# The LayerNorm bias product turned round, parts of layer 0 placed anew, and transposes of layer 1 spread over three PSUM homes

## The chip, the cores and the metric

One Trainium2 chip; the kernel runs on one core of it. The metric is the device time of one launch in microseconds (us), lower is better. The time before is 4759.32 us, the median of three runs (4757.85 to 4759.87).

## What is computed

Two layers over x of shape (2, 512, 64, 64), all in float32. Layer 0 is a Mamba layer on the 4096 tokens of each image, layer 1 matches each token with the rows of a memory of 1024 rows. Both work on a group norm of their input and add the result to it:

```python
x = x + mamba(gn(x), ln_w, ln_b, in_proj_w, conv_w, ...)
# mamba: xn = layernorm(x) * ln_w + ln_b;  xin, z = split(xn @ in_proj_w.T)
#        u = silu(conv4(xin) + conv_b);    dt, B, C = split(u @ x_proj_w.T)
#        delta = softplus(dt @ dt_proj_w.T + dt_proj_b)
#        h = exp(delta * A) * h + delta * u * B;  y = sum_n(h * C) + D * u   # along the tokens
#        out = (y * silu(z)) @ out_proj_w.T
x = x + memory(gn(x), m)
# memory: score = unit(x) @ unit(m).T;  idx = argmax(score)
#         new_m = 0.999 * m + 0.001 * (mean of the tokens of each row)
#         out = softmax(score) @ new_m
```

ln_w and ln_b are folded away: the weight `win` is multiplied by ln_w along its rows, and the vector `beta` = in_proj_w @ ln_b (from the unscaled weight) is added behind the projection.

## The kernel before, in words

**Layer 0.** Channels lie on the partitions; the tokens are cut into 32 chunks of 256 (16 for each image). A chunk has 32 *units*: 8 blocks `db` of 128 inner channels by 4 groups `g` of 4 state indices. One turn of the main loop handles unit k: `decay(k+1)` has ScalarE (ACT) write four exponentials into a PSUM tile `dA0` or `dA1`; `scan(k)` runs the recurrence on VectorE (DVE) over that tile; `weigh` multiplies by C (on DVE, or, for the units listed under `aside`, on GpSimd, POOL); `gather` has TensorE (PE) add the 8 transposed pieces into the PSUM tile `yT`; `feed(k+4)` has POOL write `bu` = B * du into one of four buffers, and `first(k+3)` has ACT write its first column. `start` prepares a pair of blocks on POOL, `turn` transposes the pair's sum back into the PSUM tile `py`, and `gate` multiplies by z.

All other work of a chunk (group norm, LayerNorm, in-projection `u_mm` and `z_mm`, convolution, softplus, out-projection) is cut into small parts, and the table `AT` says at which unit each part is issued; keys with a 1 at the end hold for chunk 1, whose front runs beside chunk 0. Layer 0 goes through `InOrder`: each engine executes its instructions in program order, so a part that waits holds up everything behind it on its engine. Layer 1's first half is not wrapped in this way, and its order on an engine can differ from the program's.

**Layer 0's start.** x is read once for the statistics of image 0 (16 loads `xl` of 512 KB through 8 buffers, DVE takes `bn_stats` of each), with the first half of `win` in the middle of these loads on SyncE's queue (SP). `affine_mm(0)` computes the first half of `beta` with `win` as the stationary operand: 8 blocks by 4 channel blocks, one moving column each. `affine_out(0)` copies it and scales that half of `win` on ACT. Behind it in program order come the end of the group statistics (`stats_end(0)`: `gs_pm`, `gs_pv` on PE, then `gsh`), the norms of chunk 0, its front, `affine_mm(1)` in two pieces, `feed(0)` to `feed(3)`, `decay(0)` and the loop. `affine_out(1)` is issued from the table at unit 0 and scales the second half of `win` on DVE; `z_mm` reads that half.

**Layer 1, first half.** Tokens come in tiles of 512, each in two pairs of 128-token sub-tiles. For a pair, seven half-size products (`product`, line 1224; the Strassen-Winograd form with banks A to D) give 256 by 1024 scores. `best` finds the row, `match` and `add_rows` add the token to a table in DRAM (gather, add, scatter through POOL's queue), `weights` and `scale` form the softmax `ex`, and `exT_part` transposes `ex` four blocks at a time into a PSUM bank, which ACT copies to `exT`. The transposes of earlier sub-tiles are done in steps 4, 5, 6 and 6 of a pair: three of them in the single bank `px`, the last one (`alt`) in the single bank `pt`, which `turn` also uses. The pool `pe` has two buffers, used by `match` (`pr`) and `add_rows` (`pe`).

**Layer 1, second half** (again in program order). `table_rows` loads both tables, 16 loads on ACT's queue; `new_m` forms a block of new memory rows on DVE; the first sums over the kept tiles `T[0]` (DVE) and `kept2` (POOL) are issued ahead of `new_m` on their engines; then products of 16 instructions follow each other on PE to the end.

Of the kernel before, what the change touches and what calls it, by code (L numbers as in the profile page):

```python
# [51 lines left out]
def kernel(  # L52
# [138 lines left out]
    with ExitStack() as l0:  # L191
# [5 lines left out]
            "u": (-10, -8, -3, 1), "xi": (-9, -6, 2, 2), "c": (-6, -2, 3, 5), "o": (-4, -1, 4, 7),  # L197
            "x": 10, "xo": 12, "z": (17, 18, 20, 23), "zo": (19, 20, 21, 24),
            "soft": (19, 21, 22, 22, 23, 24, 25, 26), "silu": 9, "aside": (0, 4, 8, 12, 16, 26),
            "gate": 2, "norm": (-3, 0, 2, 8, 9, 11, 12, 14, 16, 17, 18, 19),  # L200
            "back": ((0, 6, 8, 10, 12, 13), (1, 13, 14, 16, 17, 21)), "end": 23,
            "u1": (3, 5, 8, 9), "xi1": (4, 6, 9, 11), "c1": (6, 10, 11, 11),
            "o1": (8, 11, 12, 13), "x1": 14, "xo1": 16, "silu1": 13, "gate1": 7,
            "z1": (1, 1, 4, 5),
            "soft1": ((-7, -5, -4, -2, -1, 2, 3), (1, 4, 5, 5, 6, 8, 8), (7, 8, 8, 10, 18, 19, 19)),
            "wo": (6, -5, 8, 7), "m": (7, 12, 17, 24, 26, 29), "gs": 11, "zo1": (2, 4, 5, 6),
            "norm1": (0, 0, 0, 0, 0, 0, 0, 1, 1), "affine": 0,
            "aside_end": (2, 17, 21, 25, 27, 29),
# [38 lines left out]
        def win_load(h):  # L247
            nc.sync.dma_start(
                win[:, :, h * DI : (h + 1) * DI],
                in_wT[:, h * DI : (h + 1) * DI].rearrange("(cb p) j -> p cb j", p=P),  # L250
            )
# [115 lines left out]
        for n, xl in enumerate(stats_load(0)):  # L367
            big.append(xl)
            if n == CB * NQ // 2 - 1:
                win_load(0)  # L370
# [28 lines left out]
        pbs = {}  # L399

        def affine_mm(h, js=range(DB)):
            if js[0] == 0:
                pbs[h] = psy.tile([P, HT, 2, P], F32, tag="yT", name="pb")
                pbs[h] = pbs[h].rearrange("p a b q -> p (a b q)")
            pb = pbs[h]
            for j in js:
                for cb in range(CB):
                    nc.tensor.matmul(
                        pb[:, j : j + 1], win[:, cb, (h * DB + j) * P : (h * DB + j + 1) * P],
                        lnb[:, cb : cb + 1], start=cb == 0, stop=cb == CB - 1,  # L410
                    )

        def affine_out(h, cbs=range(CB)):
            if cbs[0] == 0:
# [633 lines left out]
        for k, (i, db, g) in enumerate(units):  # L1048
            w = k % U
            if k + 1 < n_units:  # L1050
                decay(k + 1)
# [528 lines left out]
```

## Time and profile before

The profiled execution took 4760.57 us, of which the span from its first to its last instruction is 4758.9 us.

| Stage | us from the span's start | PE busy | DVE busy | ACT busy | POOL busy |
|---|---|---|---|---|---|
| chunk 0 from its first scan | 98.30 to 206.00 | 94.56 | 74.30 | 76.60 | 84.76 |
| chunk 1 | 206.00 to 320.00 | 105.00 | 108.71 | 102.58 | 108.21 |
| a later chunk | 2461.41 to 2574.97 | 104.75 | 109.05 | 102.84 | 111.04 |
| layer 1, first half, a stretch | 3800 to 4000 | 193.72 | 164.12 | 102.60 | 96.90 |
| layer 1, second half, a stretch | 4400 to 4600 | 200.00 | 63.83 | 8.10 | 44.59 |

Times of one instruction stand on the page as "busy, mean ns"; "idle before" is what the engine waited just before the instruction, and the name behind the arrow is what ended that wait. A float32 matrix product is two instructions on PE, a transpose is one.

### The profile page before, as it was taken

What the parts mean: (1) busy time and instruction counts of PE and PEld (TensorE: products, weight loads), DVE (VectorE), ACT (ScalarE), POOL (GpSimd) and SP (SyncE); (2) the same over time, 40 slices, a digit from 0 to 9 for tenths busy, and PEclk for the clock granted to TensorE, in tenths of its full rate; (3) what the DMA queues carried; (4) which work ended last, traced back from release to release, by engine and by line L of the source; (5) the groups of instructions that cost most, each with busy time, mean ns of one, the idle gap of its engine ahead of it and who ended that gap; (6) DMA issues with size and microseconds to landing.
All of it is one profiled execution on the core that took longest, in us unless ns stands there. A gap on an engine that the chain in (4) does not pass through costs nothing. (4 is left out here: it accounts for less than half of the span.)

```text
span 4758.9 us, 65491 instructions
## 1 busy us (share of the span) xinstructions
PE 4364.2 (92%) x22644; PEld 3433.4 (72%) x22644; DVE 4157.1 (87%) x3498; ACT 3622.1 (76%) x9313; POOL 3959.6 (83%) x2664
## 2 busy tenths in 40 slices
PE   7899999999999999989999999999997699999999
PEld 6787788788877887878888878888786644454444
DVE  5799999999999999999999999999999888887322
ACT  3799899989999999889899899898988655553000
POOL 4799999999999999999999999999999744554212
PEclk9999999999999999999999999999998899999999
DMA  6132222222222222212222212222222134445442
GB/s 226 39 110 80 69 67 67 67 73 73 76 75 72 72 72 72 72 67 68 67 68 67 67 68 74 78 77 78 75 70 90 54 129 166 146 163 184 166 182 106
DMA packets 175363, 439.36 MB, mean 92 GB/s; under 512 B 23704, under 2 KB 78104, under 8 KB 171320
## 3 DMA queue, kind: packets, MB, share of 16 engines
q1 hardware_dynamic: 158072, 358.50, 22.2%
q10 hardware_dynamic: 6720, 42.08, 2.4%
q0 software_dynamic: 10240, 34.61, 2.2%
q8 instruction: 178, 2.92, 0.3%
q14 instruction: 153, 1.25, 0.1%
HBM read 347.44 MB, written 87.69 MB: 91 GB/s over the span
## 5 line engine op out<-in xcount | busy, mean ns | idle before, releaser
L38 POOL TENSOR_TENSOR bu<-B,du 128x1020 f32<-128x1020 f32 (+1 forms) x1151 | 2463.7, 2161 | 130.9 <-DVE dA L38 80.0
L38 ACT ACTIVATE dA<-delta,A 128x256 f32<-128x256 f32 x4096 | 1958.3, 478 | 131.9 <-DVE hc L38 25.6
L38 DVE TENSOR_TENSOR_SCAN dA<-dA,bu 128x1024 f32<-128x1024 f32 x832 | 1904.6, 2289 | 76.9 <-ACT dA L38 50.9
L38 PE MATMUL yT<-ident,hc 128*128 128x128 f32 x8192 | 1061.6, 277 | 148.3 <-DVE hc L38 118.9
L38 PEld LDWEIGHTS yT<-ident,hc 128*128 128x128 f32 x8192 | 932.9, 143 | 275.2 <-DVE hc L38 163.2
L38 DVE TENSOR_TENSOR hc<-dA,C 128x1024 f32<-128x1024 f32 x832 | 1016.3, 1222 | 100.7 <-PE yT L38 30.5
L38 PE MATMUL pz<-x,win 128*128 128x256 f32 x4096 | 941.7, 384 | 1.2 <-ACT z L38 1.2
L38 PEld LDWEIGHTS pz<-x,win 128*128 128x128 f32 x4096 | 771.7, 193 | 98.8 <-ACT z L38 1.4
L38 PE MATMUL po<-z,wo 128*128 128x256 f32 x2048 | 467.7, 381 | 7.1 <-ACT xd L38 6.3
L38 POOL TENSOR_TENSOR hc<-h,C 128x1024 f32<-128x1024 f32 x192 | 464.4, 2419 | 5.4 <-PE yT L38 5.4
L38 PE MATMUL cv<-xi,cd 128*128 128x256 f32 x2048 | 466.7, 380 | 1.1 <-ACT gs_d L38 1.1
L38 DVE TENSOR_TENSOR_SCAN h<-dA,bu 128x1024 f32<-128x1024 f32 x192 | 437.7, 2280 | 2.3 <-POOL hc L38 2.3
L38 PEld LDWEIGHTS po<-z,wo 128*128 128x128 f32 x2048 | 382.5, 191 | 61.1 <-ACT xd L38 11.8
L38 PEld LDWEIGHTS cv<-xi,cd 128*128 128x128 f32 x2048 | 377.9, 189 | 59.7 <-ACT dA L38 8.9
L38 POOL TENSOR_TENSOR xt<-xt,cd 128x1024 f32<-128x1024 f32 x32 | 74.5, 2348 | 274.8 <-issue 165.9
L38 ACT COPY carry<-dA 128x4 f32<-128x4 f32 x780 | 123.9, 159 | 228.9 <-DVE hc L38 228.6
L38 PE MATMUL py<-ident,ys 128*128 128x128 f32 x512 | 88.4, 299 | 175.4 <-DVE q L38 138.3
L38 ACT COPY bu<-bu 128x4 f32<-128x4 f32 x1024 | 205.3, 201 | 23.1 <-POOL bu L38 23.1
L38 PEld LDWEIGHTS py<-ident,ys 128*128 128x128 f32 x512 | 58.0, 149 | 203.4 <-ACT ys L38 191.4
L1190 POOL DMA_INDIRECT tab<-rows,ix x64 | 70.3, 1098 | 146.0 <-DVE rows L1188 97.5
L38 POOL TENSOR_TENSOR q<-q,e 128x512 f32<-128x512 f32 x127 | 162.6, 1280 | 22.3 <-ACT q L38 10.7
L38 POOL TENSOR_TENSOR delta<-delta,q 128x512 f32<-128x512 f32 x127 | 164.6, 1296 | 0.0
(241 smaller groups left out, 5986.4 us busy)
## 6 DMA issues: line engine op xcount, KB each, us to landing
B<-bcd SPq DMA_DIRECT2D x128, 512.0 KB, 4.1
C<-bcd SPq DMA_DIRECT2D x128, 512.0 KB, 4.0
wo<-in_out_wT_dram SPq DMA_DIRECT2D x128, 512.0 KB, 5.0
exd<-exT ACTq DMA_DIRECT2D x14, 2048.0 KB, 7.1
exT<-exd SPq DMA_DIRECT2D x12, 2048.0 KB, 11.9
xl<-in_x_dram SPq DMA_DIRECT2D x32, 512.0 KB, 7.5
x<-in_x_dram SPq DMA_DIRECT2D x32, 512.0 KB, 6.0
xo<-in_x_dram SPq DMA_DIRECT2D x64, 256.0 KB, 4.8
```

Of the source, the lines that this page charges most:

```text
L38: ins = call(*args, **kwargs)
L1190: nc.gpsimd.indirect_dma_start(tab, at, rows, None)
```

## The change

In words, part by part:

- **The start.** `win` is loaded behind all 16 loads of x, in four pieces for each half. The product for `beta` has ln_b as the stationary operand (one column) and 512 columns of `win` as the moving one: 8 products for each half, summed in one PSUM row in the tile `dA0` or `dA1`. ACT copies the row (`affine_row`), and 8 products with a single partition turn it into a column (`affine_turn`). Half 0: all four pieces of `win` are scaled on ACT ahead of the row's copy. Half 1: two pieces are scaled on DVE, two on POOL, behind the feeds and ahead of the loop; the turn is issued from the table at unit 0.
- **The table.** `u` of the last pair one unit earlier, the first softplus part (`d_mm`) and the first variance product one unit later, the last chunk with four `aside` units instead of six, other values for chunk 1's front, and later loads of two blocks of the out-projection.
- **The order in `decay`.** The first column of `bu` is written behind the first of four exponentials instead of ahead of them.
- **Layer 1, first half.** The transposes of steps 4, 5, 6, 6 go to `px`, `pt`, `px`, `pe`; the tail cycles through three homes or alternates between two.
- **Between the halves.** The tile `low` takes the place of `T[0]` in a pool of its own that exists from the beginning of layer 1; the first sums are cut in two halves of the tokens; the second table is loaded on SP's queue into a pool of its own. The list `e_ahead` is empty.

```diff
@@ -194,18 +194,17 @@
         AT = {
-            "u": (-10, -8, -3, 1), "xi": (-9, -6, 2, 2), "c": (-6, -2, 3, 5), "o": (-4, -1, 4, 7),
+            "u": (-10, -8, -3, 0), "xi": (-9, -6, 2, 2), "c": (-6, -2, 3, 5), "o": (-4, -1, 4, 7),
             "x": 10, "xo": 12, "z": (17, 18, 20, 23), "zo": (19, 20, 21, 24),
-            "soft": (19, 21, 22, 22, 23, 24, 25, 26), "silu": 9, "aside": (0, 4, 8, 12, 16, 26),
-            "gate": 2, "norm": (-3, 0, 2, 8, 9, 11, 12, 14, 16, 17, 18, 19),
+            "soft": (20, 21, 22, 22, 23, 24, 25, 26), "silu": 9, "aside": (0, 4, 8, 12, 16, 26),
+            "gate": 2, "norm": (-3, 0, 2, 8, 9, 11, 13, 14, 16, 17, 18, 19),
             "back": ((0, 6, 8, 10, 12, 13), (1, 13, 14, 16, 17, 21)), "end": 23,
-            "u1": (3, 5, 8, 9), "xi1": (4, 6, 9, 11), "c1": (6, 10, 11, 11),
-            "o1": (8, 11, 12, 13), "x1": 14, "xo1": 16, "silu1": 13, "gate1": 7,
-            "z1": (1, 1, 4, 5),
-            "soft1": ((-7, -5, -4, -2, -1, 2, 3), (1, 4, 5, 5, 6, 8, 8), (7, 8, 8, 10, 18, 19, 19)),
-            "wo": (6, -5, 8, 7), "m": (7, 12, 17, 24, 26, 29), "gs": 11, "zo1": (2, 4, 5, 6),
-            "norm1": (0, 0, 0, 0, 0, 0, 0, 1, 1), "affine": 0,
-            "aside_end": (2, 17, 21, 25, 27, 29),
+            "u1": (3, 5, 9, 10), "xi1": (4, 6, 9, 10), "c1": (6, 10, 11, 11),
+            "o1": (8, 10, 12, 13), "x1": 14, "xo1": 17, "silu1": 13, "gate1": 6,
+            "z1": (1, 1, 2, 5),
+            "soft1": ((-7, -5, -5, -2, -1, 2, 3), (1, 3, 4, 5, 5, 6, 8), (7, 8, 8, 10, 18, 19, 19)),
+            "wo": (6, -5, 11, 13), "m": (7, 12, 16, 24, 25, 29), "gs": 11, "zo1": (1, 3, 5, 6),
+            "norm1": (0, 0, 0, 0, 0, 0, 0, 0, 1), "affine": 0, "aside_end": (2, 17, 20, 26),
         }
@@ -245,10 +244,11 @@
         def win_load(h):
-            nc.sync.dma_start(
-                win[:, :, h * DI : (h + 1) * DI],
-                in_wT[:, h * DI : (h + 1) * DI].rearrange("(cb p) j -> p cb j", p=P),
-            )
+            for cb in range(CB):
+                nc.sync.dma_start(
+                    win[:, cb, h * DI : (h + 1) * DI],
+                    in_wT[cb * P : (cb + 1) * P, h * DI : (h + 1) * DI],
+                )
@@ -366,8 +366,7 @@
             big.append(xl)
-            if n == CB * NQ // 2 - 1:
-                win_load(0)
+        win_load(0)
         n0, n1 = ([fn for _, fn in norms(i)] for i in range(2))
@@ -397,31 +396,49 @@
         pbs = {}
-
-        def affine_mm(h, js=range(DB)):
-            if js[0] == 0:
-                pbs[h] = psy.tile([P, HT, 2, P], F32, tag="yT", name="pb")
-                pbs[h] = pbs[h].rearrange("p a b q -> p (a b q)")
-            pb = pbs[h]
-            for j in js:
-                for cb in range(CB):
+        HW = DI // 2
+
+        def affine_mm(h, cbs=range(CB)):
+            if cbs[0] == 0:
+                pbs[h] = psa.tile([P, NG, T], F32, tag=f"dA{h}", name="pb")
+                pbs[h] = pbs[h].rearrange("p n t -> p (n t)")
+            for cb in cbs:
+                for w in range(2):
                     nc.tensor.matmul(
-                        pb[:, j : j + 1], win[:, cb, (h * DB + j) * P : (h * DB + j + 1) * P],
-                        lnb[:, cb : cb + 1], start=cb == 0, stop=cb == CB - 1,
-                    )
-
-        def affine_out(h, cbs=range(CB)):
-            if cbs[0] == 0:
-                nc.scalar.copy(beta[:, h * DB : (h + 1) * DB], pbs.pop(h)[:, :DB])
+                        pbs[h][:1, w * HW : (w + 1) * HW], lnb[:, cb : cb + 1],
+                        win[:, cb, h * DI + w * HW : h * DI + (w + 1) * HW],
+                        start=cb == 0, stop=cb == CB - 1, skip_group_check=True,
+                    )
+
+        def affine_row(h):
+            row = t2.tile([P, NG, T], F32, tag="hc", name="row")
+            row = row.rearrange("p n t -> p (n t)")
+            nc.scalar.copy(row[:1], pbs.pop(h)[:1])
+            pbs[h] = row
+
+        def affine_turn(h):
+            row = pbs.pop(h)
+            pb = ps.tile([P, 2, T], F32, tag="mm", name="pt")
+            pb = pb.rearrange("p a t -> p (a t)")
+            for j in range(DB):
+                nc.tensor.matmul(
+                    pb[:, j : j + 1], row[:1, j * P : (j + 1) * P], ident[:1, :1],
+                    start=True, stop=True,
+                )
+            nc.scalar.copy(beta[:, h * DB : (h + 1) * DB], pb[:, :DB])
+
+        def affine_scale(h, cbs, engine=None):
             for cb in cbs:
                 half = win[:, cb, h * DI : (h + 1) * DI]
-                if h == 0:
+                if engine is None:
                     nc.scalar.mul(half, half, lnw[:, cb : cb + 1])
                 else:
-                    nc.vector.tensor_scalar(half, half, lnw[:, cb : cb + 1], None, ALU.mult)
+                    engine.tensor_scalar(half, half, lnw[:, cb : cb + 1], None, ALU.mult)
...
         affine_mm(0)
-        affine_out(0, range(CB // 2))
+        affine_scale(0, range(CB))
+        affine_row(0)
+        affine_turn(0)
@@ -874,7 +891,7 @@
-        def decay(k):
+        def decay(k, beside=None):
             i, db, g = units[k]
@@ -883,6 +900,8 @@
                 )
+                if n == 0 and beside is not None:
+                    first(beside)
             dAs[k] = dA
@@ -953,15 +972,13 @@
-        AHEAD = 2
         gn0, gn1, mean, centre, square0, var0, _, var1, root, newton, scale = n0
...
         gn1()
-        affine_out(0, range(CB // 2, CB))
         mean()
...
         square0()
-        affine_mm(1, range(AHEAD))
+        affine_mm(1, range(1))
         var0()
@@ -993,7 +1010,7 @@
         dl0[0].pop(0)()
-        affine_mm(1, range(AHEAD, DB))
+        affine_mm(1, range(1, CB))
         for fn in dl0[0]:
@@ -1011,7 +1028,10 @@
-        table = [(AT["affine"], 0, lambda: affine_out(1))]
+        affine_scale(1, range(CB // 2), nc.vector)
+        affine_scale(1, range(CB // 2, CB), nc.gpsimd)
+        affine_row(1)
+        table = [(AT["affine"], 0, lambda: affine_turn(1))]
         for p in range(PR):
@@ -1048,7 +1068,7 @@
             if k + 1 < n_units:
-                decay(k + 1)
+                decay(k + 1, k + LEAD - 2 if 0 < k and k + LEAD - 2 < n_units else None)
             if w % (2 * G) == 0 and k > 0:
@@ -1064,8 +1084,6 @@
                 feed(k + LEAD)
-            if k + LEAD - 1 < n_units:
-                first(k + LEAD - 1)
             if (k + 5) % (2 * G) == 0 and k + 5 < n_units:
@@ -1083,6 +1101,9 @@
     p3 = ctx.enter_context(tc.tile_pool(name="q3", bufs=2))
+    ahead = ctx.enter_context(tc.tile_pool(name="ahead", bufs=1))
+    low = ahead.tile([P, K // P // 2, TT], F32, name="low")
+    e_ahead = [ahead.tile([P, ROW], F32, name=f"e1_{kb}") for kb in range(0)]
     kept = {}
@@ -1151,13 +1172,11 @@
-        def exT_part(ex, exT, i, kh, alt=False):
-
-            if alt:
-                px = ps_t.tile([P, C], F32, tag="pt", name="px2")
-                px = px.rearrange("p (q k) -> p q k", k=P)
-            else:
-                px = ps_x.tile([P, KBH, P], F32, tag="px", name="px")
+        def exT_part(ex, exT, i, kh, home="px"):
+
+            pool = {"px": ps_x, "pt": ps_t, "pe": ps_e}[home]
+            px = pool.tile([P, TT], F32, tag=home, name="px")
+            px = px.rearrange("p (q k) -> p q k", k=P)
             for q in range(KBH):
@@ -1228,10 +1247,10 @@
-        def transpose_late(kh, alt=False):
+        def transpose_late(kh, home="px"):
             if late:
                 ex, exT, i, k, stored = late[0]
-                exT_part(ex, exT, i, kh, alt)
+                exT_part(ex, exT, i, kh, home)
                 if kh == KH - 1:
@@ -1302,9 +1321,9 @@
                 if step in (4, 5, 6) and go:
-                    transpose_late(step % 2)
+                    transpose_late(step % 2, "pt" if step == 5 else "px")
                 if step == 6 and go:
-                    transpose_late(1, True)
+                    transpose_late(1, "pe")
@@ -1356,33 +1375,39 @@
         for kh in range(3 * KH):
-            transpose_late(kh % KH, kh % 2 == 1)
+            transpose_late(kh % KH, ("px", "pt", "pe")[kh % 3])
         sels[1] = match(*behind[1])
         for kh in range(KH):
-            transpose_late(kh, kh % 2 == 1)
+            transpose_late(kh, ("px", "pt")[kh % 2])
         sels[0] = match(*behind[0])
...
         for kh in range(KH):
-            transpose_late(kh, kh % 2 == 1)
+            transpose_late(kh, ("px", "pt")[kh % 2])
         add_rows(*behind[0], sels[0])
...
             for kh in range(KH):
-                transpose_late(kh, kh % 2 == 1)
+                transpose_late(kh, ("px", "pt")[kh % 2])
...
         p_e = s.enter_context(tc.tile_pool(name="p_e", bufs=KB))
+        p_f = s.enter_context(tc.tile_pool(name="p_f", bufs=KB - len(e_ahead)))
         ps_o = s.enter_context(tc.tile_pool(name="qo", bufs=1, space=PSUM))
...
             for i, tab in enumerate(tabs):
-                e.append(p_e.tile([P, ROW], F32, tag=f"e{i}", name=f"e{i}"))
-                nc.scalar.dma_start(e[i], tab[kb * P : (kb + 1) * P])
+                if i == 1 and kb < len(e_ahead):
+                    e.append(e_ahead[kb])
+                else:
+                    pool = (p_e, p_f)[i]
+                    e.append(pool.tile([P, ROW], F32, tag=f"e{i}", name=f"e{i}"))
+                queue = (nc.scalar, nc.sync)[i]
+                queue.dma_start(e[i], tab[kb * P : (kb + 1) * P])
             return e
@@ -1428,7 +1453,7 @@
         def tile_sums(b1, b2, engine, first):
-            T = [r1.tile([P, QH, TT], F32, tag=f"T{n}", name=f"T{n}") for n in (1, 2, 4)]
+            T = [low] + [r1.tile([P, QH, TT], F32, tag=f"T{n}", name=f"T{n}") for n in (2, 4)]
             first.tensor_sub(T[0], b2[:, half[0]], b1[:, half[0]])
@@ -1455,10 +1480,13 @@
         lds = [load_pair(0), load_pair(1)]
-        T = [r1.tile([P, QH, TT], F32, tag=f"T{n}", name=f"T{n}") for n in (1, 2, 4)]
+        T = [low] + [r1.tile([P, QH, TT], F32, tag=f"T{n}", name=f"T{n}") for n in (2, 4)]
         ts = T
-        nc.vector.tensor_sub(T[0], kept2[:, half[0]], kept1[:, half[0]])
-        nc.gpsimd.tensor_sub(kept2[:, half[0]], kept2[:, half[1]], kept2[:, half[0]])
+        for h in range(2):
+            t = slice(h * 2 * P, (h + 1) * 2 * P)
+            b21, b22 = kept2[:, half[0], t], kept2[:, half[1], t]
+            nc.vector.tensor_sub(low[:, :, t], b21, kept1[:, half[0], t])
+            nc.gpsimd.tensor_sub(b21, b22, b21)
         for kb in range(KB):
```

## The prediction

> **What bounds the kernel now.** I read the busy times by stage first, to see which engine has no room left in each.
>
> ```profile
> 98.30:206.00 107.70, 94.56 (x493) 80.77 (x494) 74.30 (x52) 76.60 (x196) 84.76 (x61) 0.94 0.02 6
> ...
> 2461.41:2574.97 113.56, 104.75 (x618) 90.97 (x617) 109.05 (x71) 102.84 (x271) 111.04 (x71) 1.00 0.21 71
> ...
> 3800.00:4000.00 200.00, 193.72 (x664) 99.68 (x665) 164.12 (x358) 102.60 (x233) 96.90 (x99) 1.00 0.41 141
> 4400.00:4600.00 200.00, 200.00 (x467) 88.54 (x466) 63.83 (x43) 8.10 (x8) 44.59 (x20) 1.00 0.45 171
> ```
>
> The columns are stretch, length, PE, weight loads, DVE, ACT, POOL, clock, DMA. A chunk of the main loop is full on DVE (109.1 of 113.6) and on POOL (111.0). Chunk 0 is not: PE is nearest with 94.6 of 107.7. Layer 1 is bound by PE, its second half without a gap. So a part placed elsewhere in the main loop can only win back waits of DVE and POOL. The waits and the timeline of that chunk show them:
>
> ```profile
> DVE dA L38 <- ACT dA L38: 37.4, 20, 1.9
> DVE hc L38 <- PE yT L38: 12.3, 14, 2.2
> POOL bu L38 <- DVE dA L38: 61.5, 40, 2.4
> ACT bu L38 <- POOL bu L38: 18.0, 26, 1.1
> ...
> 2574.97 2.30 DVE L38 TENSOR_TENSOR_SCAN dA<-dA,bu 128x1024 f32<-128x1024 f32 x1 [1.87 <-ACT dA L38]
> ```
>
> (Total us, times, longest, from 400 to 3500.) DVE's wait of 1.87 us comes once in a chunk, two units behind ACT's silu: table load 1.28, silu 1.91 and 1.99, table load 1.28. POOL's wait is its echo. The change leaves these ACT instructions as they are.
>
> Then the start, in order of time:
>
> ```profile
> 21.47 13.78 PE L38 MATMUL pb<-lnb,win 128*128 128x1 f32 x64 [21.47 <-DMA win<-in_in_wT_dram]
> 22.64 10.27 DVE L38 BATCH_NORM_STATS2 st<-xl 128x6 f32<-128x512 f32 x16 [4.95 <-DMA xl<-in_x_dram]
> 35.12 0.57 PE L38 MATMUL gs_pm<-gs_w,gmat 128*128 128x4 f32 x2
> 39.53 2.07 ACT L38 ACTIVATE x<-x,gsh,grs 128x256 f32<-128x256 f32 x4 [1.31 <-DVE gsh L38]
> 40.18 3.46 PE L38 MATMUL pm<-x,meanc 128*128 128x256 f32 x8 [3.07 <-ACT x L38]
> 82.50 8.93 PE L38 MATMUL pb<-lnb,win 128*128 128x1 f32 x48
> ```
>
> The statistics (DVE, done at 32.9) and the product (PE, done at 35.25) end close together; the group norm waits for the product only because `gs_pm` stands behind it on PE. Last, the waits of PE in layer 1 and the step between its halves:
>
> ```profile
> PE px L1163 <- ACT exT L1164: 10.6, 17, 1.0
> PE A L38 <- DVE win L38: 9.2, 1, 9.2
> ...
> 4360.82 4.49 POOL L38 TENSOR_TENSOR exT<-exT 128x2048 f32<-128x2048 f32 x1 [4.33 <-issue]
> 4361.93 3.93 DVE L38 TENSOR_TENSOR e<-e,e 128x513 f32<-128x513 f32 x1 [1.25 <-DMA e<-tab]
> 4367.18 9.15 PE L38 MATMUL A<-exT,win 128*128 128x512 f32 x16 [9.25 <-DVE win L38]
> ```
>
> PE waits 10.6 us in all for the one `px` bank, and 9.25 us at the boundary, where the first table sum takes 3.93 us beside POOL's subtraction; the next such sum (4366.95) takes 0.69.
>
> **The start, step by step.** Loads: eight `xl` come about 1.3 us apart (six `bn_stats` pairs, 7.34 to 15.01), so 16 of them land by 7.3 + 15 x 1.3 = 26.8, and the statistics end near 28.2, 4.6 us earlier. The half of `win` (2.1 MB, at the 400 GB/s of 21 to 32 us: 5.2) now lands in pieces from 28.2 to 32.1, against 21.4. Product: 16 instructions of 512 columns. A layer 1 product has 4 in 1.72 us, 0.43 each: 6.9 us. But PE is slow this early: the 8 of `pm` above take 3.46 us, later ones (147.91) 1.89. All at half speed would be 13.7. I take four slow and twelve full, 8.6 us, because the in-projection at 49.1 runs 32 in 7.53, full speed, after some 8 us of dense work. End 36.8. Then, in line: the last scaling (1.09), the row's copy (1.01, as the copy of A at 4376.42), and the turn, 16 instructions at 0.123 (`pb` at 43.48: 16 in 1.97 with weight loads) to 0.215 (64 in 13.78), 2.0 to 3.4, taken 2.5. `gs_pm` starts at 41.4 instead of 35.1: **+6.3 us** (+4.2 with 6.9 and 2.0; +12.4 with 13.7 and 3.4). All of it is on the path: gsh, norm of x, mean, variance, in-projection follow each other, and PE is then full from 60 to 80.
>
> [...]
>
> Second half: 48 instructions in 8.93 become 12 x 0.43 = 5.2, -3.8 (at 0.86: +1.4); the turn adds 2.5 (2.0 to 3.4) ahead of chunk 1's mean, whose consumer on DVE stands ahead of the first scan. **-1.3 us** (-1.8 to +4.8). Scaling on POOL: 128x1024 with a scalar per partition is not in the trace. `cd<-cd,gmu,grs` takes 2.08 for 512, so 4.1; with immediates (line 1114) 0.62, so 1.2. Two of them are 2.5 to 8.3 us; I take 8.3, the row with scalars per partition. They stand behind three feeds (93.60, 7.25 us) and `z_mm(0)` (103.4) waits for them, with the gathers behind it on PE. With the delay so far the feeds end near 107 and the scaling at 115, against 108 for `z_mm(0)`: 7 us late, of which I charge half since chunk 0 leaves PE 13 us idle: **+3.5** (0 to +7). The other values for chunk 1's front act on the same 13 us: taken **-5** (-10 to +3). DVE's two scalings fewer (1.4) lie beside the wait for the mean. Start: 6.3 - 1.3 + 3.5 - 5 = **+3.5** (-8 to +27).
>
> **The main loop: -1 us** (-5 to +6). The first column behind the first exponential: ACT's 18.0 us of waits for POOL come once a chunk (0.59 at 2500.44), where DVE runs on without a gap, so nothing; where ACT is late (2572.67), the sum of carry, column and four exponentials is the same in both orders. `u_mm(3)` moves past four small `yT` products only (2537.85), since `py` holds PE before both. `d_mm` moves behind a gather of 0.9 us; its reader on ACT comes 4.3 us later (2493.8, 2498.0). That lets the gather start 1.1 us earlier, worth a little of the 12.3 us. If the reader became late, ACT and then DVE would wait; 3 us are left.
>
> **The last chunk: -2 us** (-5 to +3). Without `aside` at its units 27 and 29, DVE no longer waits 0.94 and 1.34 for POOL's `hc` (3780.25, 3787.40) and does two products more (1.13 each); PE is full from 3779 to 3800, so what is won is what POOL gets free before. The later loads of the out-projection on SP are far from use.
>
> **Layer 1, first half: -9 us** (-10.6 to +5). Step 6 no longer waits for the copy of step 5, which stands on ACT behind a 1.15 us exponential. The cover of the new homes: `pt` is copied 2 to 3 us before `turn` needs it, `pe` before the next `add_rows`.
>
> **The boundary: -4 us** (-5.5 to +2). `low` needs no tile of the first half, so half of the first sums can go ahead; POOL's second half (4.49 / 2) ends by about 4361, and the first table sum takes 0.69 instead of 3.93, some 3.2 us; the rest is one issue (0.55) less ahead of the second load. PE behind it is gapless, so this arrives at the end in full.
>
> Sum: 3.5 - 1 - 2 - 9 - 4 = -12.5; 4760.6 - 12.5 = 4748.1. The profiled execution lies 1.25 above the median, so **4747 us** on the scale of the runs.
>
> **Rivals.** First, slower: *the start eats everything*. PE stays at half speed for lack of work (+12.4 and +4.8), the POOL scaling counts in full (+7) and the placements win nothing (+3): +27 instead of +3.5, giving 4770. It decides from +19 on, where the other terms (-16) are spent and 3 more lost. For it: the `pb` row; against: 512 columns keep PE far busier than one. Second, *layer 1 gives nothing*: `pe` is freed by a DVE sum that waits for a gather from DRAM (55.4 us in 15 waits), so the next `pr` waits instead of the next transpose: 4747 + 9 = 4756. Against: `pr` comes 8 us behind that product (4109.57, 4118.59), the sum about 2.5 us behind it. Third, *chunk 0 closes its gaps*: DVE is idle 33 us there; with the placements at -10 and a start without POOL's 3.5, the main loop at -5 and the rest as above: 4747 - 12.5 = 4734.
>
> **How the numbers follow.** Forecast 0.55, first rival 0.15, second 0.15, third 0.15. I call a difference under 0.2%, 9.5 us, no change, about what a measurement of this kernel can tell; the bounds are then 4749.8 and 4768.8. The forecast's own range is 4738 to 4755, with 0.40 of its 0.55 below 4749.8; with the third rival faster has 0.55. The forecast's other 0.15, the second rival and 0.02 of a milder first make 0.32 for the same; 0.13 is left for slower. The range 4729 to 4766 leaves out the ends of the first and third.
>
> **What would show it.** `gs_pm` near 41 and the first scan 4 to 8 us behind 98.31; chunks still 113.6 us apart with the same 1.87; no PE wait on `px`; a first table sum of 0.7 us and `A` within 6 us of the last transpose. Chunks shorter by over 0.5 us, or a first scan ahead of 98, would prove me wrong.

## The result, and the profile after

The changed kernel takes 4794.13 us (median of 6 runs, 4792.61 to 4797.45), the kernel before 4759.15 us (6 runs, 4755.88 to 4760.26) beside it. The ratio is 1.0074, with a 95% interval of 1.0064 to 1.0084: 35 us slower, where 12 us faster was forecast. The profiled execution of the changed kernel has a span of 4793.5 us, 34.6 us more than the 4758.9 before.

Where the 34.6 us lie is read from the starts of the 1024 scans on DVE, 32 to a chunk (chunks are counted from 0), and from the first product of layer 1:

| stage | before, us | after, us | difference |
|---|---|---|---|
| first scan starts | 98.31 | 106.89 | +8.6 |
| chunk 0 | 143.53 | 142.08 | -1.5 |
| chunk 1 | 114.44 | 121.36 | +6.9 |
| chunks 2 to 30 | 3317.64 | 3352.40 | +34.8 |
| chunk 31 to the first product of layer 1 | 133.00 | 129.72 | -3.3 |
| layer 1, first half and boundary | 560.26 | 549.25 | -11.0 |
| layer 1, second half | 391.68 | 391.78 | +0.1 |

So the start, the last chunk and layer 1 together win 7.1 us, where 11.5 were forecast for them, and the main loop (chunks 1 to 30) loses 41.7. The stages of the changed kernel, in the columns stretch, length, PE, weight loads, DVE, ACT, POOL, clock, DMA:

```profile
106.89:214.59 107.70, 95.28 (x500) 81.20 (x501) 76.04 (x53) 78.04 (x201) 91.30 (x63) 0.93 0.02 6
2488.34:2604.39 116.05, 107.45 (x618) 93.55 (x617) 109.16 (x71) 102.80 (x271) 111.15 (x71) 0.97 0.21 69
3850.00:4050.00 200.00, 197.37 (x672) 100.88 (x671) 167.01 (x366) 104.74 (x241) 101.50 (x102) 1.00 0.42 144
4440.00:4640.00 200.00, 200.00 (x467) 88.54 (x466) 68.22 (x44) 8.10 (x8) 43.76 (x19) 1.00 0.44 171
```

The second row is one steady chunk. DVE and POOL do the same work as before (109.2 and 111.2 us, against 109.1 and 111.0), but the chunk takes 116.05 us instead of 113.56. PE is 2.7 us longer at work for as many products, and its clock has gone from 1.00 to 0.97. The waits from 400 to 3500 us name the victim:

```profile
DVE hc L38 <- PE yT L38: 49.3, 45, 3.4
DVE dA L38 <- ACT dA L38: 48.4, 31, 1.9
```

DVE's wait for `yT` has grown from 12.3 to 49.3 us. Its wait behind the silu is there as before: before, 8 of these waits stand under POOL's `bu`, and the two groups sum to 50.6 us there, 48.4 here.

In order of time, the places that the prediction spoke of:

```profile
28.11 9.47 PE L38 MATMUL pb<-win,lnb 128*1 128x512 f32 x16 [28.11 <-DMA win<-in_in_wT_dram]
43.19 0.59 PE L38 MATMUL gs_pm<-gs_w,gmat 128*128 128x4 f32 x2
98.43 3.57 PE L38 MATMUL pt<-ident,row 1*128 1x1 f32 x16 [2.83 <-ACT row L38]
105.75 1.22 DVE L38 TENSOR_TENSOR x<-x,pm 128x1024 f32<-128x1024 f32 x1 [6.25 <-PE pm L38]
106.89 2.28 DVE L38 TENSOR_TENSOR_SCAN h<-dA,bu 128x1024 f32<-128x1024 f32 x1
108.38 5.66 POOL L38 TENSOR_SCALAR win<-win,lnw 128x1024 f32<-128x1024 f32 x2
308.89 5.41 PE L38 MATMUL po<-z,wo 128*128 128x256 f32 x16 [4.00 <-DMA wo<-in_out_wT_dram]
4399.69 0.70 DVE L38 TENSOR_TENSOR e<-e,e 128x513 f32<-128x513 f32 x1 [3.48 <-DMA e<-tab]
4401.70 9.01 PE L38 MATMUL A<-exT,win 128*128 128x512 f32 x16 [9.00 <-DVE win L38]
```

`gs_pm` is 8.1 us later than before. In chunk 1 PE waits 4.00 us for a weight load that was moved. At the boundary the first table sum takes 0.70 us, as forecast, but it now waits 3.48 us for its rows, and `A` waits 9.00 us instead of 9.25.

**The clock.** The next view of the changed kernel cuts part of a steady chunk into steps of 3.413 us, laid where the clock record changes (columns as above):

```profile
2558.93:2562.34 3.41, 3.32 (x20) 2.74 (x18) 3.31 (x3) 3.31 (x9) 2.62 (x2) 1.00 0.71 254
2562.34:2565.75 3.41, 1.09 (x8) 0.86 (x8) 3.41 (x3) 3.31 (x11) 3.41 (x3) 1.00 0.48 127
2565.75:2569.16 3.41, 3.16 (x10) 2.75 (x11) 3.32 (x3) 2.99 (x9) 3.41 (x2) 0.50 0.94 328
2569.16:2572.57 3.41, 3.41 (x23) 3.12 (x22) 3.00 (x3) 3.06 (x10) 3.41 (x3) 1.00 0.06 22
2603.31:2606.72 3.41, 3.26 (x20) 2.42 (x18) 2.30 (x1) 3.31 (x10) 1.14 (x1) 1.00 0.18 62
2606.72:2610.13 3.41, 2.02 (x12) 1.53 (x12) 3.31 (x2) 3.04 (x9) 3.36 (x2) 1.00 0.62 169
2610.13:2613.54 3.41, 3.41 (x11) 2.90 (x11) 3.41 (x5) 3.34 (x10) 3.37 (x7) 0.50 0.65 49
2613.54:2616.95 3.41, 3.41 (x18) 3.00 (x17) 2.86 (x2) 2.84 (x8) 3.41 (x2) 1.00 0.38 124
```

Twice a step in which PE has little to do (1.09 and 2.02 us of 3.41) is followed by one whole step at half clock (from here on "a fall"; a place with so little work is "a thin place"). Every change of the clock in this trace lies on one grid of 3.413 us (the stretches of its clock record last 3.413, 6.827, 13.653 us and so on). The kernel before has such falls too, 16 between 100 and 3600 us; the changed kernel has 42, of which 38 stand in pairs 44.37 us (13 steps) apart, pair after pair at 116.05 us, which is 34 steps. The first place of the pair is the pause ahead of the `py` transposes:

```profile
2566.00 1.09 PE L38 MATMUL py<-ident,ys 128*128 128x128 f32 x4 [1.77 <-DVE q L38]
```

The kernel before has this pause too; 12 of its 13 falls from 200 to 3600 us stand behind it at the beginning of a chunk, the other late in chunk 16. DVE's own lines in this chunk of the changed kernel are

```profile
2572.99 1.23 DVE L38 TENSOR_TENSOR hc<-dA,C 128x1024 f32<-128x1024 f32 x1 [0.82 <-PE yT L38]
2618.19 1.22 DVE L38 TENSOR_TENSOR hc<-dA,C 128x1024 f32<-128x1024 f32 x1 [1.78 <-PE yT L38]
```

One wait stands behind each fall, 2.60 us together. A chunk without a fall takes 113.51 to 113.55 us in this trace, 113.45 in the traces of a_soft19 and a_rows96 below; 113.45 + 2.60 = 116.05.

**Which part of the change opens the second place.** PE's timeline of the changed kernel there:

```profile
2608.11 1.09 PE L38 MATMUL yT<-ident,hc 128*128 128x128 f32 x8 [1.53 <-DVE hc L38]
2609.13 1.13 PE L38 MATMUL pd<-xd,wdt 33*128 33x256 f32 x4
2610.19 1.22 PE L38 MATMUL yT<-dD,u 128*128 128x128 f32 x4
2611.20 1.91 PE L38 MATMUL pv<-sq,meanc 128*128 128x256 f32 x4
```

and of the kernel before, at the same work:

```profile
2576.00 1.04 PE L38 MATMUL yT<-ident,hc 128*128 128x128 f32 x8
2576.97 1.13 PE L38 MATMUL pd<-xd,wdt 33*128 33x256 f32 x4
2578.68 1.09 PE L38 MATMUL yT<-ident,hc 128*128 128x128 f32 x8 [0.59 <-DVE hc L38]
2579.61 1.03 PE L38 MATMUL pv<-sq,meanc 128*128 128x256 f32 x4
```

Before, the four `pd` products (`d_mm`) fill part of the pause in which PE waits for DVE's `hc`. With `soft` at 20 they stand behind the next gather, and the pause is 1.53 us.

To find a bound I counted PE's work in every step from 200 to 3600 us: 0.852 ns for each column (128-column products start 0.109 us apart in both traces), doubled at half clock (there they start 0.213 us apart), as a share of the step. Counted so, the two kinds of step overlap in the changed kernel: falls follow shares up to 0.56, yet there are full-clock steps with 0.41 and no fall behind them. If each product counts by the share of the 128 rows that it contracts over (33 of 128 for `pd`, shown as `33*128`), they part: falls follow shares up to 0.376 in the kernel before and 0.366 in the changed one, and the lowest shares without a fall are 0.385 and 0.404. With this count the step from 2562.34 has 0.26, and the step from 2606.72 has 0.32 (unweighted 0.51). This is an observation; the runs below test it as a cause.

### The profile page after: what moved, and what is told of

It reads as the page before. It is cut to its first block, busy times and chain, and to the rows that moved or that the text cites. A ratio compares the mean times of both kernels' runs of the same rounds, so it can differ in the third digit from the quotient of the medians.

```text
span 4793.5 us, 65349 instructions
## 1 busy us (share of the span) xinstructions
PE 4401.1 (92%) x22580; PEld 3456.0 (72%) x22580; DVE 4153.6 (87%) x3499; ACT 3617.3 (75%) x9315; POOL 3968.4 (83%) x2665
## 5 line engine op out<-in xcount | busy, mean ns | idle before, releaser
L38 PE MATMUL yT<-ident,hc 128*128 128x128 f32 x8192 | 1044.3, 277 | 159.4 <-DVE hc L38 136.7
L38 DVE TENSOR_TENSOR hc<-dA,C 128x1024 f32<-128x1024 f32 x834 | 1019.3, 1222 | 133.2 <-PE yT L38 65.4
L38 PE MATMUL pz<-x,win 128*128 128x256 f32 x4096 | 955.8, 388 | 0.0
L38 PEld LDWEIGHTS po<-z,wo 128*128 128x128 f32 x2048 | 395.7, 196 | 60.1 <-DMA wo<-in_out_wT_dram 4.2
L38 ACT COPY bu<-bu 128x4 f32<-128x4 f32 x1024 | 186.3, 182 | 4.7 <-POOL bu L38 4.6
L38 PEld LDWEIGHTS yT<-dD,u 128*128 128x128 f32 x1024 | 157.3, 204 | 39.9 <-issue 31.7
```

Of the source, the lines that this page charges most:

```text
L38: ins = call(*args, **kwargs)
```

## The experiments

The theory, from here on "the clock trap": the one number that moves `d_mm` opens a second thin place on PE, and the falls there, and not the new order as such, cost the 35 us. Falls are counted from 100 to 3600 us in the profiled run of each kernel; "mean chunk" is that of chunks 3 to 30. Each group of four shares its runs of the kernel before, to which the ratios refer: their medians are 4758.63 (a_soft19, a_rows96, b_soft20, a_wo), 4756.35 (b_l1, b_fill, b_start, best1) and 4757.34 us (b_dummy, b_l1r, best2, b_homes). The mean granted clock of every single run, profiled or not, agrees with the falls of the profiled one: 0.972 to 0.973 in all runs of after, b_soft20 and a_wo, 0.980 to 0.985 in those of a_soft19 and a_rows96, 0.982 to 0.984 before, 0.986 to 0.989 in b_dummy.

| kernel | us | ratio to before (95%) | falls | mean chunk, us |
|---|---|---|---|---|
| before | 4759.15 | | 16 | 114.43 |
| after | 4794.13 | 1.0074 (1.0064 to 1.0084) | 42 | 115.67 |
| a_soft19 | 4756.33 | 0.9997 (0.9988 to 1.0007) | 16 | 114.33 |
| a_rows96 | 4748.66 | 0.9982 (0.9972 to 0.9991) | 13 | 113.98 |
| b_soft20 | 4805.59 | 1.0098 (1.0081 to 1.0115) | 43 | 115.89 |
| a_wo | 4789.68 | 1.0067 (1.0050 to 1.0084) | 41 | 115.54 |
| b_l1 | 4743.03 | 0.9972 (0.9961 to 0.9983) | 16 | 114.31 |
| b_fill | 4763.30 | 1.0013 (1.0003 to 1.0022) | 17 | 115.02 |
| b_start | 4762.24 | 1.0013 (1.0004 to 1.0023) | 16 | 114.19 |
| best1 | 4742.43 | 0.9966 (0.9952 to 0.9980) | 15 | 114.20 |
| b_dummy | 4743.12 | 0.9973 (0.9963 to 0.9982) | 3 | 113.87 |
| b_l1r | 4731.95 | 0.9948 (0.9931 to 0.9964) | 13 | 114.13 |
| best2 | 4728.50 | 0.9939 (0.9923 to 0.9956) | 2 | 113.95 |
| b_homes | 4744.68 (one run) | | 17 | 114.30 |

**The number put back (a_soft19).** The changed kernel with

```diff
-            "soft": (20, 21, 22, 22, 23, 24, 25, 26),
+            "soft": (19, 21, 22, 22, 23, 24, 25, 26),
```

> The changed kernel with one number put back: the delta product (d_mm) issues at unit 19 of its pair again, not at 20. Theory (clock trap): in the changed kernel the granted clock falls to half for one step of 3.41 us twice in most chunks, 44.4 us apart, and chunks take 116.05 us; the second fall stands where d_mm moved behind a gather, so that PE has little to do around it. With d_mm back, that place goes: falls come at most once in two or three chunks, as in the kernel before (15 between 100 and 3600 us, against 42), the steady chunks take 113.6 to 114.5, and the 35 us lost between chunk 3 and the last come back: 4755 to 4762. Rival 1 (the first column behind the first exponential slows the chunk): no change, 4790 to 4797. Rival 2 (d_mm's own lateness makes DVE wait, clock or not): 4755 to 4762 as well; the next run tells it apart.

4756.33 us: 38 us less than the changed kernel, and no difference from the kernel before. The falls are back at 16. Rival 1 is out as the cause of the loss; rival 2 forecast the same and stands.

**The same order, more rows (a_rows96).** The changed kernel with

```diff
-        wdt = wp.tile([R + 1, DI], F32, name="wdt")
+        wdt = wp.tile([XO + 2 * N, DI], F32, name="wdt")
+        for r in range(R, XO + 2 * N, 32):
+            nc.gpsimd.memset(wdt[r : r + 32], 0.0)
...
-                        s["pd", p][:, j], wdt[:, db * P : (db + 1) * P], s["xd"][: R + 1],
+                        s["pd", p][:, j], wdt[:, db * P : (db + 1) * P], s["xd"],
```

> The changed kernel with the same order of work; only the delta product contracts over 96 rows, 33 as before and 63 of zeros in the weight, instead of over 33. It has as many instructions of the same shape, which take the same time. Theory (clock trap, with the activity counted by rows): weighted with the share of active rows, PE's work in the 3.41 us step before a fall is at most 0.38 in every fall of both traces, and at least 0.385 in every step that no fall follows; unweighted the two overlap (0.41 to 0.56). With 96 rows the step around the delta product comes above it, so the second fall goes: falls 44 us behind the first vanish, chunks 113.6 to 114.5, 4755 to 4762. Rival 2 (the order of instructions itself makes DVE wait): 4790 to 4797, as the order is the changed kernel's. Rival 1: the same, 4790 to 4797.

4748.66 us: 45 us less than the changed kernel, from multiplying 63 rows of zeros, and 6 under my interval. The order on PE is the changed kernel's, down to the pause:

```profile
871.61 1.09 PE L38 MATMUL yT<-ident,hc 128*128 128x128 f32 x8 [1.53 <-DVE hc L38]
872.54 1.03 PE L38 MATMUL pd<-xd,wdt 96*128 96x256 f32 x4
873.41 0.61 PE L38 MATMUL yT<-dD,u 128*128 128x128 f32 x4
873.85 1.03 PE L38 MATMUL pv<-sq,meanc 128*128 128x256 f32 x4
```

A grid step of this run reaches from 869.84 to 873.25. With 33 rows its share would be 0.33, with 96 it is 0.44, and the step behind it keeps the full clock (columns as in the views of stages):

```profile
869.84:873.25 3.41, 1.88 (x15) 1.56 (x14) 3.28 (x3) 3.07 (x8) 2.97 (x2) 1.00 0.68 209
873.25:876.66 3.41, 3.41 (x19) 3.05 (x18) 3.41 (x5) 3.31 (x11) 3.37 (x6) 1.00 0.44 42
```

In this trace five steps would have been under the bound with 33 rows and are above it with 96; no fall follows any of them. So rival 2 is out too: it is not the order that makes DVE wait, but the clock that falls in it. Rows also save 7.7 us against a_soft19: chunks 8 to 16, which do the products for M and the group statistics beside, sum to 1027.5 us against 1037.6.

**The number alone (b_soft20).** The kernel before with the reverse of the first diff.

> The kernel before with d_mm one unit later (19 to 20) and nothing else. Theory (clock trap): the one number is enough to open the second place; the chunks fall into step with 34 windows of 3.413 us (116.05 us) in long stretches, and the time is 4780 to 4800. Rival 1 (something else of the new order slows the chunks): 4756 to 4763, no change. A middle value, 4765 to 4775, would mean that the number opens the second place, but that another edit is needed to hold the chunks in step.

4805.59 us, 47 us more than the kernel before and above my interval: the number is enough, and does worse alone, without the gain of layer 1 beside it. 43 falls; chunks 1 to 11 and most of 18 to 29 take 115.6 to 116.4 us.

**The weight load (a_wo).** The changed kernel with

```diff
-            "wo": (6, -5, 11, 13),
+            "wo": (6, -5, 8, 7),
```

> The changed kernel with the weight loads of the out-projection at their old places (8 and 7 instead of 11 and 13). In chunk 1 PE waits 4.00 us for the last of them at 308.89, and the scans lose 5.4 us there. Theory: this wait goes, and 4 to 5.5 us come back: 4788 to 4791, with chunk 0 to 2 as much shorter. Rival: what is won there is lost again in the next chunks, as the chunks fall into step with the clock's windows anyway: 4792 to 4797.

4789.68 us, 4.4 less than the changed kernel. The wait for `wo` in chunk 1 is gone, and chunk 1 takes 116.09 us, against 121.36, 121.86 and 122.11 in the three traces with the moved load (after, a_soft19, a_rows96). So the moved load was not free in chunk 1. The start of chunk 2 moves from 370.33 to 366.21; but in this trace the first scan is 4.4 us earlier too (102.48) and chunk 0 5.6 us longer, so the 4.4 us of the total are not the load's alone.

**Layer 1 alone (b_l1).** The kernel before with layer 1 of the changed kernel.

> The kernel before with layer 1 of the changed kernel (three homes for the transposes, low outside the first half's tiles, the table loads split over two queues); layer 0 is that of the kernel before. In the trace of the changed kernel the way from the first product of layer 1 to the end is 11.0 us shorter (first half with the boundary 560.3 to 549.3, second half 391.7 to 391.8). Theory (that is what layer 1 is worth, whatever layer 0 does): 4745 to 4751. By the forecast's terms (-9 and -4): 4746. Rival (part of it comes only from layer 0's later end, as loads have more time there): 4752 to 4758.

4743.03 us, 13.3 less, and 2 under my interval. The way from the first product of layer 1 to the first of its second half is 548.4 us in this trace (560.3 before), so 11.9 us are layer 1's own; the rest is within the spread of the runs.

**The homes alone (b_homes).** Of layer 1, only `exT_part` with its three pools and its calls; `low` and the split of the table loads are left as before.

> The kernel before with the three homes of the transposes alone, without low outside the first half's tiles and without the split of the table loads. Read from its trace: the way from the first product of layer 1 to the first of its second half, 560.3 us before, 549.3 in the changed kernel. Theory (the boundary gives next to nothing: A waits 9.00 instead of 9.25 us, as the last scatter to the table now ends it): 549 to 551, and A's wait 11 to 13 us, as transposes that end sooner only wait longer for the table; the split and low then win 2 to 4 of it back. Rival (the table is not late): A's wait stays at 9.2 and the way is 551.

The same way takes 548.49 us with the homes alone and 548.42 us with all of layer 1. So `low` and the split give 0.1 us, less than my 2 to 4, and `A` waits 9.9 us, less than the 11 to 13 I expected. PE's waits in layer 1, from 3840 to 4420 us, in the run with the homes alone:

```profile
PE A L38 <- DVE win L38: 9.9, 1, 9.9
PE px L1161 <- ACT exT L1162: 1.6, 4, 1.0
```

Without the split, the first table sum starts at 4345.44 us and takes 3.96 beside POOL; with it (b_l1), it starts at 4349.44 and takes 0.69. Counted from the first product of layer 1 (3802.22 and 3803.04), it ends after 547.2 us in the one and 547.1 in the other. The rows of the first sum come from two loads; in the changed kernel the SP queue starts its eight at 4392.78, the ACT queue its first at 4394.74, and the DMA engines are then busy to 0.89 and more. That the rows come late because the other queue's loads were ahead is argued, not shown.

**The start alone (b_start).** The kernel before with the changed kernel's loads and bias product; placements, first column and layer 1 as before.

> The kernel before with the start of the changed kernel alone (loads in the new order, bias product with the weight as moving side, scalings on DVE and POOL); all placements, the first column and layer 1 are those of the kernel before. Theory (the start is a delay that the main loop doesn't give back): the first scan at 104 to 108 instead of 98.3 to 99.7, chunk 1 begins 4 to 9 us later, no wait of PE for wo in chunk 1, steady chunks with falls as in the kernel before: 4763 to 4769. By the forecast's terms without the placements (6.3 - 1.3 + 3.5): 4767. Rival (the start is nearly free, since chunk 0 leaves PE idle): 4757 to 4762.

4762.24 us, 5.9 more than before: between my interval and the rival's, so the run does not part them. The first scan is at 106.26, chunk 1 begins 9.4 us later than in the kernel before, just beyond the 4 to 9 that I expected, and PE does not wait for `wo` in chunk 1. In this trace chunks 1 to 16 are 6.8 us shorter than before, 4.0 of it in chunk 16 alone; the start costs some 6 us net.

**Work moved into the other pause (b_fill).** The kernel before, with this in the loop over the units, and the last `u_mm` cut into two halves of 8 products:

```diff
+            if w == 0 and i in halves:
+                halves.pop(i)()
             if w % (2 * G) == 0 and k > 0:
                 turn(*((i, w // (2 * G) - 1) if w else (i - 1, PR - 1)))
```

> The kernel before; of the last in-projection product of each chunk's front (16 instructions), the first 8 are issued one step earlier on PE, ahead of the four py transposes that wait 1.77 us for the copy of yT. Theory (clock trap): this pause is the one place of a steady chunk where PE's work in 3.41 us is under the bound (0.26; 1.4 us of the 3.41 us of phases), and it brings the falls that the kernel before has. 1.8 us of useful work in it lift the place above the bound: at most 6 falls between 100 and 3600 us instead of 15 or 16, chunks of 113.5 throughout instead of a mean of 114.4, and 15 to 24 us less: 4735 to 4744. Rival (a fall in the clock costs nothing here, since DVE and POOL are full): 4755 to 4761. Against both: if the half product holds py up, DVE's gate is late and it is slower than 4761.

4763.30 us, 7 more than before: a miss, in the wrong direction. PE's timeline shows why (the profiled run, at 4775.80 us, is the slowest of the ten):

```profile
2549.31 1.89 PE L38 MATMUL pz<-x,win 128*128 128x256 f32 x8
2551.24 0.63 PE L38 MATMUL py<-ident,ys 128*128 128x128 f32 x4
2551.71 0.61 PE L38 MATMUL yT<-dD,u 128*128 128x128 f32 x4
2552.16 1.89 PE L38 MATMUL pz<-x,win 128*128 128x256 f32 x8
2554.68 1.09 PE L38 MATMUL yT<-ident,hc 128*128 128x128 f32 x8 [0.63 <-DVE hc L38]
2556.91 3.44 PE L38 MATMUL yT<-ident,hc 128*128 128x128 f32 x15 [1.14 <-POOL hc L38]
```

The wait ahead of `py` is gone, but PE has no more work than before: the pause comes back behind the second half, as 0.63 and 1.14 us. The falls go on (17), and 10 of them last two steps or more, where the kernel before has 3 such of 16: the steady chunks with a longer fall take 116.2 to 117.1 us, those with a fall of one step 114.4 to 114.8, as before.

**Work added to the pause (b_dummy).** The kernel before, with 8 products of the identity with itself ahead of `py`:

```diff
+        def idle_work(i):
+            pz = ps.tile([P, 2, T], F32, tag="mm", name="pz")
+            for _ in range(8):
+                nc.tensor.matmul(
+                    pz[:, 0, :P], ident, ident, is_transpose=True, start=True, stop=True,
+                )
...
+            if w == 0 and 0 < i < last:
+                idle_work(i + 1)
             if w % (2 * G) == 0 and k > 0:
                 turn(*((i, w // (2 * G) - 1) if w else (i - 1, PR - 1)))
```

> The kernel before with added work and nothing taken away: in each chunk from the second to the last but one, 8 products of the identity with itself (128 columns, 0.109 us each by the yT rows, 0.87 us in all) stand on PE ahead of the four py transposes, in the pause of 1.77 us; they write the bank that the next in-projection product overwrites. The half product of the run before only moved the pause behind itself (PE waits of 0.63 and 1.14 us behind it); added work leaves the order behind it as it was. Theory (clock trap): PE's work around the pause rises from 0.26 to at least 0.45 of a step at every phase, so no steady chunk has a fall: at most 9 falls between 100 and 3600 us instead of 16, the steady chunks all at 113.55, mean chunk 113.7 to 114.0 instead of 114.43, and 12 to 20 us less: 4736 to 4745, although the kernel does more. Rival 1 (falls cost nothing unless in step): 4754 to 4759. Rival 2 (PE's time counts there): 30 x 0.87 = 26 us more, up to 4782.

4743.12 us, 14 less than the kernel before, though the kernel does more. The added products run in the pause:

```profile
2519.75 1.09 PE L38 MATMUL yT<-ident,hc 128*128 128x128 f32 x8 [0.88 <-DVE hc L38]
2520.68 1.04 PE L38 MATMUL pz<-ident 128*128 128x128 f32 x8
2522.61 0.63 PE L38 MATMUL py<-ident,ys 128*128 128x128 f32 x4 [0.90 <-DVE q L38]
2523.53 3.62 PE L38 MATMUL pz<-x,win 128*128 128x256 f32 x16
```

3 falls are left, and the chunks from 17 to 30 take 113.4 to 113.6 us, but for one of 113.9. Both rivals are out: the falls had a price in the kernel before as well, without any chunk in step, and PE's time did not count there.

**Put together (best1, b_l1r, best2).** best1 is the kernel before with layer 1, 96 rows and the half product of b_fill.

> The kernel before with layer 1 of the changed kernel, the half product ahead of py, and the delta product over 96 rows (zeros below the 33). Theory: the three gains add: 11 (layer 1), 15 to 24 (no falls at py), and some 3 to 6 where the delta product over 33 rows is next to a pause in the chunks with extra work (chunk 16 took 116.13 instead of 120.85 with 96 rows): 4718 to 4732. Rival (the falls cost nothing unless in step): 4745 to 4750.

4742.43 us: a miss, 10 above the theory's range and 3 under the rival's, and no better than layer 1 alone (4743.03). That the half product takes back what the rows give is argued from b_fill and b_l1r, not shown by itself. b_l1r is the kernel before with layer 1, 96 rows, and the first column behind the first exponential:

> The kernel before with layer 1 of the changed kernel, the first column behind the first exponential, and the delta product over 96 rows. Layer 1 alone gave 4743. Theory: the first column is worth 0.1 us a chunk (steady chunks without a fall take 113.45 in the changed kernel and 113.55 in the kernel before), 3 us; the 96 rows take away the falls of the chunks with extra work, 5 to 8 us: 4731 to 4737. Rival (the 96 rows only help where d_mm stands late): 4738 to 4743.

4731.95 us, as forecast; chunks without a fall take 113.45 instead of 113.55. best2 is b_l1r with the 8 added products:

> The run above with the 8 products in the pause. Theory: the gains add, hardly a fall is left between chunk 2 and the last but one, mean chunk 113.5 to 113.7: 4716 to 4728. Rival (96 rows and added products mend the same falls): 4729 to 4737.

4728.50 us, the fastest of all, 29 us less than the kernel before and 66 less than the changed one. That is between my interval and the rival's: against b_l1r it wins 3.5 us for 11 falls fewer, where a fall cost some 1 us each before. In the profiled runs chunks 1 to 30 are 6.1 us shorter than in b_l1r, and chunk 31, which the edit leaves alone, is 4.2 longer. Two falls are left, but the mean chunk is 113.95 and not 113.5 to 113.7: chunks 9 to 15 still take 113.9 to 114.5 us; what they wait for beside the clock is open.

Over the traces of all 14 kernels, from 200 to 3600 us, the bound by rows holds: 247 falls follow shares up to 0.400, and the 13,408 steps at full clock without a fall behind them have 0.385 or more, so the two meet in a narrow band, with 7 of each kind in it. Unweighted, falls follow shares up to 0.59, and 604 of the steps without a fall lie below that. The transposes, the 8 added products of b_dummy among them, are counted in full here like any product.

## Why the prediction was wrong

**The main loop** was put at -1 us (-5 to +6) and is +41.7 (chunks 1 to 30). Two of the steps behind that failed.

The first is the sentence on `d_mm`, "behind a gather of 0.9 us; its reader on ACT comes 4.3 us later". It priced the move by who waits for the product, and nobody is held up by it; what the move took away was PE's work in a pause, and PE's clock fell there. I priced the loop from one chunk of 113.56 us with a clock of 1.00, and did not ask why chunks 3 to 30 of the same trace have a mean of 114.43. A good part of the answer was in the trace of before: 12 falls in these chunks, worth some 1 us each, nearly all at the one thin place that it had. (The rest lies in chunks 8 to 16 with their extra work: b_dummy, with hardly a fall, still has a mean of 113.87.) The premise that a part placed elsewhere "can only win back waits of DVE and POOL" left out that it can also bring new ones, through PE's clock. The price of the step is 38 us by a_soft19, 45 by a_rows96, and 47 the other way round by b_soft20.

The second stands under the last chunk: "The later loads of the out-projection on SP are far from use". In chunk 1 they are not: PE waited 4.00 us there, and chunk 1 is some 5 us longer than with the old places (a_wo).

**The first column** behind the first exponential was called worth nothing; 0.1 us a chunk (113.55 to 113.45) is 3 us over the loop. **u_mm(3)** was not tried alone.

**The start** was +3.5 (-8 to +27), and is +7.1 at the end of chunk 0; alone +5.9. Over all traces chunk 1 begins at 239.8 to 244.2 us with the old start and at 245.9 to 251.3 with the new one, so single traces fix this to a few us only. `gs_pm` came 8.1 us later, not 6.3: the product took 9.47 us instead of 8.6, since its first six instructions stand 0.80 to 0.85 us apart, not four, and the others 0.43. That four would be slow was my estimate, and no run shows it. The turn took 3.46 instead of 2.5, its upper end, with products 0.21 us apart while the granted clock stood at 0.50 (39.9 to 53.6 us). The second half was put at -1.3, and is +1.9 (from +6.7 at `xd` to +8.6 at the first scan): its turn took 3.57, again at 0.50 (97.9 to 115.0 us), and I left out that PE waits 2.83 us for ACT's copy of the row. POOL's two scalings took 5.66 us instead of 8.3. The two terms of chunk 0, +3.5 for POOL and -5 for the placements, sum to the -1.5 that was measured; but chunk 0 takes 142.1 to 147.6 us in the five traces with the new start, and the placements were not tried alone, so this agreement may be luck.

**The last chunk**, -2, is -3.3, but chunk 31 takes 128.9 to 133.2 us in the ten traces with its old placements and 125.7 to 129.7 in the four with the new ones, and they were not tried alone. **Layer 1's first half**, -9, was right in its cause: the waits for `px` fell from 10.6 to 1.4 us, and the homes alone shorten the way by 11.8. That is 1.2 beyond my bound of -10.6; where the 2.8 us beyond the waits for `px` come from is open. **The boundary**, -4, is 0: the first sum is 3.2 us shorter, as worked out, but starts later. I took the rows as there, and did not follow the loads, which the change moves to another queue.

**The rivals.** The start did not eat everything; layer 1 did give; chunk 0 did not close its gaps. The slower side of my range had only the start as a mechanism. The sign that I named, chunks still 113.6 us apart, was the right one to look at: they are 116.05. Without the clock trap the forecast would still have been 9 us too low: a_soft19 is at 4756.33, no faster than the kernel before. In its trace the start (+4.1 at the beginning of chunk 1) and chunk 1 (+7.4) spend what layer 1 (-11.2) and the last chunk (-3.3) win. That a_rows96, at 4748.66, lies near the forecast of 4747 is luck: it holds 7.7 us from the rows, a gain that no term of mine had.

## What to carry to other kernels

PE was not the bound of the main loop here and still set its pace through its clock: a steady chunk took 116.05 us with two falls and 113.45 to 113.55 without one. So before moving a product that nobody waits for, count what PE has left to do in each clock step around the place it leaves, by columns and by rows (in these traces falls followed shares up to 0.400, and steps without one had 0.385 or more). A chunk time that varies while its work does not is worth a look at the clock column in steps as fine as its own: the 0.97 of the steady chunk hid two steps at 0.50. Moving useful work into a thin place only moved the pause here (b_fill, 7 us slower); adding rows or products to it, where PE was not the bound, was faster than the leaner kernel (a_rows96 by 45 us, b_dummy by 14).

## What was not expected of the hardware

A fall did not take an idle step. The clock fell behind steps in which PE worked up to 0.40 of the time by the row count, with no single pause over 1.8 us at the two places of the steady chunk (1.77 and 1.53 us). A pause of 1.53 us was enough where thin products of 33 rows stood behind it, and the same pause was not with 96 rows (a_rows96).

Rows count. A product over 33 rows took as long as one over 96 (1.13 us for four at 33 rows, 1.03 at 96), but did less to hold the clock: 42 falls with 33 rows (after), 13 with 96 (a_rows96).

The falls kept in step with the loop. A chunk with both falls takes 34 steps (116.05 us), so the next chunk meets the grid at the same two places, and the changed kernel stays there for twelve chunks on end (18 to 29). It left the first such stretch (chunks 3 to 8) where the products for M begin beside (chunk 8); b_soft20 stays in its first one to chunk 11, so these alone do not end it. Why the length comes out at 34 steps so exactly was not tried.
